# A Mamba-style scan on one Trainium2 core: in the last pair of images VectorE takes five of eight products with C instead of four

## The chip, the cores and the metric

The kernel runs on one core of one Trainium2 chip. The metric is the device time of a run in microseconds; the kernel before has a median of 14022.91 us over three runs (14009.71 to 14023.95). Five engines of the core matter: TensorE (PE in the profile; its weight loads are PEld), VectorE (DVE), ScalarE (ACT), GpSimd (POOL) and SyncE (SP), which here only issues DMAs. Each engine runs its own queue of instructions in a fixed order and waits on semaphores for the others.

## The reference, cut to what matters

Four layers are applied in turn to eight images of 64 channels and 64 x 64 points: a self-attention over points with convolutions, two windowed attention blocks, a decoupled dynamic filter, and a selective scan (SS2D) with a small modulation network behind it. The change lies in the selective scan of the fourth layer. For every image there are K = 4 directions, 128 inner channels, N = 16 states and a sequence of L = 4096 points:

```
def step(h, inp):
    u_t, dt_t, B_t, C_t = inp
    h = h * jnp.exp(dt_t[..., None] * A) + dt_t[..., None] * B_t[:, :, None, :] * u_t[..., None]
    return (h, jnp.einsum('bkcn,bkn->bkc', h, C_t))
```

So each state n has its own recurrence along the points, h = h * exp(dt * A) + (dt * u) * B, and the output is the sum over the states of h * C. B and C depend on the point and the state but not on the channel.

## The kernel before, in words

Channels lie on the 128 partitions. Images are worked in four pairs. The main program (`tile_kernel`, L1838) runs, for each pair, the method `scans` (L1619); between the steps of the scans it takes pieces of other work from a generator: the part behind the scans of the pair before (`back`, L1755) and the layers in front of the scans of the pair to come (`front`). In the last pair there is no pair to come, so only `back` of the third pair is mixed in, and after the last scan its own `back` runs alone.

A pair has two images, four directions and eight chunks of 512 points: 64 units (the list `units`, L1629). A unit has eight steps (`i % 8`), and a step treats two of the 16 states, j = 0 and j = 1. That is 512 steps for a pair and 2048 in all. The scans of the last pair are steps 1536 to 2047; below, unit numbers count from the start of that pair, so that units 0 to 31 are its first image and 32 to 63 its second.

What one step needs, and which engine does it:

- `fetch` (L1677): SP issues a DMA that broadcasts two rows of B, and another for two rows of C, to all partitions, 512 KB each. B is fetched three steps ahead and C two steps ahead. The tiles of B and of C have three buffers each, so a fetch waits until the product that reads the same buffer three steps earlier has ended; SP issues its DMAs strictly in order.
- `products` (L1684), two steps ahead: POOL multiplies both rows of B with dt * u into the tile `vd` (six buffers), one instruction over 128 x 1024 elements (L1687).
- `step` (L1689): for each of the two states ScalarE writes exp(dt * A) into a PSUM bank called `dad` (L1707); VectorE runs the recurrence as one scan instruction over 512 points (L1710), from `dad` and `vd`, into `to`; and ScalarE copies the last point of `to` to `carry` for the next chunk (L1718). `to` is either the SBUF tile `hd` (one buffer for even and one for odd steps) or `dad` itself, in place, so that the state stays in PSUM.
- The product with C, written over `vd`. It has two forms, chosen by `rp` (L1696). Where `rp` is 0 one POOL instruction covers both states (L1721). Elsewhere POOL multiplies the first state, which is in SBUF (L1723), and VectorE the second, which is in PSUM (L1724). In the first three pairs `rp` is set in odd steps; in the last pair (`image >= B - 2`) it is set in every step, so VectorE takes four of every eight products.
- `sums` (L1726): TensorE adds the two products of a step to the output bank `yd` with an identity matrix (L1737); after the eighth step VectorE adds `yd` to the running sum Y (L1746, L1748, L1751).

At the start of each unit `inputs` (L1653) loads the points `xs`, and forms dt and dt * u (`pdd` and `du`; L1662 to L1669) and the rows of B and C (L1671 to L1675), which go to DRAM and come back by `fetch`.

[...]Three are in the pool of the scans under the tag `da` (for `dad`, `pdd` and `pbc`), one is `yd`, three belong to the mixed-in work (tag `f`), and one to its accumulations. `bank` (L1179) hands them out. In the last pair, once the mixed-in work is used up, `turn` is set (L1645) and `bank` alternates between the two pools, so that `dad` rotates through six banks; that is so from unit 32 on.

The order of the instructions on each engine is not written out by hand. A scheduler that orders the whole program when it is built decides it, from priorities and its own estimate of durations; on the chip the order is fixed. So a change of one product can move others.

Of the kernel before, what the change touches and what calls it, by code (L numbers as in the profile page):

```python
# [11 lines left out]
ALU = mybir.AluOpType  # L12
# [3 lines left out]
B, C, HH, WW = 8, 64, 64, 64  # L16
# [9 lines left out]
NTD = L // TD  # L26
# [1121 lines left out]
class _Direct:  # L1148
# [540 lines left out]
    def step(self, i, st):  # L1689

        nc, w, net = self.nc, self.w, self.net
        wk, ps = self.sw, self.ps
        u = self.units[i // 8]
        k, c, at, CC, v = u["k"], u["c"], u["at"], st["C"], st["v"]

        n0, rp = 2 * (i % 8), i % 2 or u["image"] >= B - 2  # L1696
        rev = k >= 2

        def along(t):
            return t[:, ::-1] if rev else t  # L1700

        h = wk.tile([P, 2 - i % 2, TD], F32, name="hd", tag=f"h{i % 2}", bufs=1)
        hs = []
        for j in range(2):
            n = n0 + j
            da = self.bank("dad", (P, TD), "da")
            nc.scalar.activation(da, u["du"][:, 0], AF.Exp, scale=net.As[:, k, n : n + 1])  # L1707
            first = 0.0 if at == 0 else self.carries[:, n : n + 1]
            to = da if rp and j else h[:, j]
            nc.vector.tensor_tensor_scan(along(to), along(da), along(v[:, j]), first, ALU.mult, ALU.add)  # L1710
            hs.append(to)
            if at < NTD - 1 and (rp or j):
                ends = h[:, :, 0] if rev else h[:, :, TD - 1]
                cs = self.carries[:, n0 : n0 + 2]
                if rp:
                    ends = to[:, 0:1] if rev else to[:, TD - 1 : TD]
                    cs = self.carries[:, n : n + 1]
                nc.scalar.activation(cs, ends, AF.Copy)  # L1718

        if rp == 0:  # L1720
            st["w"] = nc.gpsimd.tensor_tensor(v, h, CC, ALU.mult)  # L1721
        else:
            st["w"] = nc.gpsimd.tensor_tensor(v[:, 0], h[:, 0], CC[:, 0], ALU.mult)  # L1723
            nc.vector.tensor_tensor(v[:, 1], hs[1], CC[:, 1], ALU.mult)  # L1724

    def sums(self, i, st, after=None):  # L1726

# [161 lines left out]
```

## Time and profile before

| what | value |
|---|---|
| median of three runs | 14022.91 us |
| the profiled execution's own time | 14012.53 us |
| its span in the profile | 14010.7 us |
| mean granted TensorE clock | 0.862 |
| start of the last pair's first product with B | 11620.8 us |
| start of the next 32 units (second image) | 12710.8 us |
| start of the last product with B | 13745.8 us |

The profile is one execution on the chip. A group of instructions is named by line, engine and operation, then output <- inputs with their sizes, how often it ran, its busy time in us and the mean of one in ns. "<-" behind a group or in a view of waits names what ended the idle time before it. Durations of neighbouring instructions of VectorE and POOL overlap by some tens of nanoseconds, so costs are better read from one start to the next. In a view by stretches of time each row gives the busy time of every engine, the granted clock, the mean busy share of the 16 DMA engines and what they moved.

### The profile page before, as it was taken

What the parts mean: (1) busy time and instruction counts of PE and PEld (TensorE: products, weight loads), DVE (VectorE), ACT (ScalarE), POOL (GpSimd) and SP (SyncE); (2) the same over time, 40 slices, a digit from 0 to 9 for tenths busy, and PEclk for the clock granted to TensorE, in tenths of its full rate; (3) what the DMA queues carried; (4) which work ended last, traced back from release to release, by engine and by line L of the source; (5) the groups of instructions that cost most, each with busy time, mean ns of one, the idle gap of its engine ahead of it and who ended that gap; (6) DMA issues with size and microseconds to landing.
All of it is one profiled execution on the core that took longest, in us unless ns stands there. A gap on an engine that the chain in (4) does not pass through costs nothing. (4 is left out here: it accounts for less than half of the span.)

```text
span 14010.7 us, 141613 instructions
## 1 busy us (share of the span) xinstructions
PE 11364.2 (81%) x46358; PEld 4240.7 (30%) x46358; DVE 8425.0 (60%) x9763; ACT 7041.2 (50%) x15460; POOL 8178.9 (58%) x4111
## 2 busy tenths in 40 slices
PE   9888979978888669988889667997998866666665
PEld 2255222234433222224433222223443222222221
DVE  0222254477766874356675767337666677997875
ACT  5533156556544645555553645555554554454442
POOL 0000046578767765556665685457666688878982
PEclk9966789989889789998899788998888878888887
DMA  0000044456555754445554675335544577878882
GB/s 17 1 1 2 6 163 162 159 185 226 195 181 189 246 195 149 135 154 176 176 177 160 227 248 172 131 132 189 173 163 166 183 253 259 273 250 275 276 273 97
DMA packets 705499, 2379.23 MB, mean 170 GB/s; under 512 B 81060, under 2 KB 81188, under 8 KB 703980
## 3 DMA queue, kind: packets, MB, share of 16 engines
q1 hardware_dynamic: 681024, 2315.57, 48.9%
q10 hardware_dynamic: 23724, 54.50, 1.0%
q8 instruction: 367, 6.01, 0.2%
q14 instruction: 384, 3.15, 0.1%
HBM read 2269.08 MB, written 100.66 MB: 169 GB/s over the span
## 5 line engine op out<-in xcount | busy, mean ns | idle before, releaser
L1687 POOL TENSOR_TENSOR vd<-B,du 128x1024 f32<-128x1024 f32 x2048 | 4841.8, 2369 | 3920.1 <-DMA B<-rows 2103.0
L1737 PE MATMUL yd<-vd,pack 128*128 128x512 f32 x8192 | 4625.9, 695 | 1265.4 <-POOL vd L1721 449.5
L1710 DVE TENSOR_TENSOR_SCAN hd<-dad,carry,vd 128x512 f32<-128x512 f32 x2464 | 3093.2, 1271 | 1146.2 <-ACT dad L1707 669.9
L1707 ACT ACTIVATE dad<-du,As 128x512 f32<-128x512 f32 x4096 | 2718.4, 680 | 1017.3 <-DVE hd L1710 701.9
L1737 PEld LDWEIGHTS yd<-vd,pack 128*128 128x128 f32 x8192 | 1624.1, 215 | 3956.6 <-issue 1863.1
L1721 POOL TENSOR_TENSOR vd<-hd,C 128x1024 f32<-128x1024 f32 x768 | 1811.7, 2359 | 1324.0 <-DVE hd L1710 695.7
L1723 POOL TENSOR_TENSOR vd<-hd,C 128x512 f32<-128x512 f32 x1280 | 1637.0, 1280 | 317.9 <-DVE hd L1710 230.0
L1277 ACT ACTIVATE e<-s 128x512 f32<-128x512 f32 x2048 | 1199.2, 591 | 1030.1 <-PE s L1271 1028.6
L1710 DVE TENSOR_TENSOR_SCAN dad<-dad,carry,vd 128x512 f32<-128x512 f32 x1120 | 1427.6, 1275 | 126.5 <-POOL vd L1687 77.5
L1271 PE MATMUL s<-X 64*128 64x512 f32 x4096 | 1343.5, 647 | 105.5 <-ACT e L1277 105.3
L1263 PE MATMUL po<-e,VT 128*64 128x512 f32 x4096 | 1155.4, 631 | 19.0 <-ACT e L1277 19.0
L1718 ACT ACTIVATE carry<-hd 128x1 f32<-128x1 f32 (+1 forms) x1792 | 357.3, 201 | 1225.9 <-DVE hd L1710 1215.5
L1724 DVE TENSOR_TENSOR vd<-dad,C 128x512 f32<-128x512 f32 x1280 | 860.9, 673 | 72.7 <-ACT carry L1718 62.4
L1425 PEld LDWEIGHTS w_av<-vals,w_e 64*64 64x64 f32 x16384 | 630.9, 163 | 204.5 <-ACT w_e L1415 99.4
L1425 PE MATMUL w_av<-vals,w_e 64*64 64x9 f32 x16384 | 658.6, 218 | 38.2 <-ACT w_e L1415 38.0
L1271 PEld LDWEIGHTS s<-X 64*128 64x128 f32 x4096 | 363.5, 187 | 1052.4 <-issue 823.7
L1710 DVE TENSOR_TENSOR_SCAN hd<-dad,vd 128x512 f32<-128x512 f32 x352 | 420.1, 1211 | 191.7 <-ACT dad L1707 88.3
L1748 DVE TENSOR_TENSOR Y<-Y,yd 128x512 f32<-128x512 f32 x128 | 124.8, 975 | 661.3 <-PE yd L1737 661.1
L1718 ACT ACTIVATE carry<-dad 128x1 f32<-128x1 f32 x1120 | 189.5, 169 | 616.6 <-DVE dad L1710 614.4
L1415 ACT ACTIVATE w_e<-w_e 128x512 f32<-128x512 f32 x512 | 310.8, 627 | 360.7 <-DVE w_e L1410 239.4
L1410 DVE TENSOR_TENSOR w_e<-w_s,bias 128x512 f32<-128x512 f32 x512 | 328.8, 682 | 236.3 <-PE w_s L1398 235.3
L1263 PEld LDWEIGHTS po<-e,VT 128*64 128x64 f32 x4096 | 212.9, 136 | 824.6 <-issue 581.0
(247 smaller groups left out, 11150.5 us busy)
## 6 DMA issues: line engine op xcount, KB each, us to landing
B<-rows SPq DMA_DIRECT2D x2048, 512.0 KB, 5.0
C<-rows SPq DMA_DIRECT2D x2048, 512.0 KB, 4.5
xs<-xt SPq DMA_DIRECT2D x128, 256.0 KB, 2.9
xs<-xc SPq DMA_DIRECT2D x128, 256.0 KB, 3.4
xc<-xcv ACTq DMA_DIRECT2D x64, 256.0 KB, 3.8
zs<-z ACTq DMA_DIRECT2D x64, 256.0 KB, 3.8
xt<-XT ACTq DMA_DIRECT2D x32, 512.0 KB, 7.8
rows<-bc SPq DMA_DIRECT2D x256, 64.0 KB, 2.0
```

The source lines that it names most:

```text
L1263: nc.tensor.matmul(po[half[im]], lhsT=VT[:, t, half[im]], rhs=es[im], start=(t == 0), stop=(t == 31))
L1271: nc.tensor.matmul(ss[im], lhsT=at(half[im], t), rhs=X[half[im], jc * CH : (jc + 1) * CH], start=True, stop=True)
L1277: nc.scalar.activation(e, ss[im], AF.Exp, scale=C**-0.5, accum_out=parts[:, im, t, jc : jc + 1])
L1425: nc.tensor.matmul(self.av[half[im], x % 4 + j, h, :], lhsT=es[h // 4][half[im], j, h % 4, :], rhs=V[half[im], x + j, h, :], start=True, s ...
L1687: self.nc.gpsimd.tensor_tensor(v, st["B"], dx.to_broadcast([P, 2, TD]), ALU.mult)
L1707: nc.scalar.activation(da, u["du"][:, 0], AF.Exp, scale=net.As[:, k, n : n + 1])
L1710: nc.vector.tensor_tensor_scan(along(to), along(da), along(v[:, j]), first, ALU.mult, ALU.add)
L1718: nc.scalar.activation(cs, ends, AF.Copy)
L1721: st["w"] = nc.gpsimd.tensor_tensor(v, h, CC, ALU.mult)
L1723: st["w"] = nc.gpsimd.tensor_tensor(v[:, 0], h[:, 0], CC[:, 0], ALU.mult)
L1724: nc.vector.tensor_tensor(v[:, 1], hs[1], CC[:, 1], ALU.mult)
L1737: m = nc.tensor.matmul(y, lhsT=w["ident"], rhs=st["v"][:, j], start=(n == 0), stop=(n == NST - 1))
```

## The change

The test is no longer a yes or no for the whole step but the number of the step's states that VectorE multiplies, `own`. In the first three pairs it is 0 in even and 1 in odd steps, as `rp` was. In the last pair it is 1 in three of four steps and 2 in every fourth (i % 4 == 3). Where it is 2, both scans write in place into their PSUM banks, both carries are copied from there, and VectorE does both products with C; POOL does none in that step, and the tile `hd` of the step is allocated but not written. So VectorE takes five of every eight products. Everything outside `step` is the same. In the changed program each engine's instructions stand in the same order as before up to the start of the last pair's scans.

```
-        n0, rp = 2 * (i % 8), i % 2 or u["image"] >= B - 2
+        n0 = 2 * (i % 8)
+        own = 1 + (i % 4 == 3) if u["image"] >= B - 2 else i % 2
...
-            to = da if rp and j else h[:, j]
+            to = da if j >= 2 - own else h[:, j]
             nc.vector.tensor_tensor_scan(along(to), along(da), along(v[:, j]), first, ALU.mult, ALU.add)
             hs.append(to)
-            if at < NTD - 1 and (rp or j):
+            if at < NTD - 1 and (own or j):
                 ends = h[:, :, 0] if rev else h[:, :, TD - 1]
                 cs = self.carries[:, n0 : n0 + 2]
-                if rp:
+                if own:
...
-        if rp == 0:
+        if own == 0:
             st["w"] = nc.gpsimd.tensor_tensor(v, h, CC, ALU.mult)
-        else:
-            st["w"] = nc.gpsimd.tensor_tensor(v[:, 0], h[:, 0], CC[:, 0], ALU.mult)
-            nc.vector.tensor_tensor(v[:, 1], hs[1], CC[:, 1], ALU.mult)
+        for j in range(2 if own else 0):
+            engine = nc.vector if j >= 2 - own else nc.gpsimd
+            m = engine.tensor_tensor(v[:, j], hs[j], CC[:, j], ALU.mult)
+            if j == 0:
+                st["w"] = m
```

## The prediction

> **What bounds the kernel now.** I read the page first. The shares of the whole span name TensorE, but the slices show that the last sixth is another regime.
>
> ```profile
> PE 11364.2 (81%) x46358; PEld 4240.7 (30%) x46358; DVE 8425.0 (60%) x9763; ACT 7041.2 (50%) x15460; POOL 8178.9 (58%) x4111
> ...
> POOL 0000046578767765556665685457666688878982
> ```
>
> The eights and nines at the end of POOL's row are the last pair's scans. Its 512 steps begin at 11620.8 and end near 13748: 2127 us, the only part where the two programs' order differs. There I asked for the busy time by stretch, cut where the products with B of step 8u start. Columns: stretch, its length, PE, PEld, DVE, ACT, POOL busy, clock, DMA share, GB/s.
>
> ```profile
> 11620.80:12139.30 518.50, 363.94 (x662) 120.61 (x662) 435.70 (x445) 265.37 (x618) 455.70 (x255) 0.89 0.81 279
> 12139.30:12552.40 413.10, 278.90 (x474) 93.73 (x473) 391.57 (x431) 218.11 (x445) 323.12 (x179) 0.81 0.69 239
> 12552.40:12740.00 187.60, 121.89 (x216) 39.44 (x216) 151.84 (x158) 88.25 (x209) 170.35 (x97) 0.88 0.85 294
> 12740.00:12983.60 243.60, 156.77 (x257) 53.90 (x257) 183.29 (x186) 105.36 (x247) 200.47 (x115) 0.80 0.76 256
> 12983.60:13748.20 764.60, 493.44 (x852) 171.75 (x852) 610.40 (x620) 346.88 (x831) 678.93 (x382) 0.85 0.81 275
> 13296.00:13330.50 34.50, 20.90 (x33) 7.21 (x34) 27.41 (x29) 15.90 (x40) 28.45 (x18) 0.80 0.73 240
> 13330.50:13358.70 28.20, 18.63 (x40) 6.46 (x38) 23.51 (x24) 14.00 (x35) 28.20 (x16) 1.00 0.96 322
> ```
>
> The last two rows are two neighbouring units of eight steps. The second is solid POOL: 28.20 of 28.20. The first does the same work in 34.5 us. The static order explains it: in one unit VectorE takes each step's two scans in turn ("straight"); in the other it runs the second states' scans of steps 2 to 6 ahead of the first states' ("crossed"), so POOL's product with C of step 2 stands waiting. The second image's 24 units from 12983.6 on are 12 of each: 12 x 34.4 + 12 x 28.25 = 752, and 13 us more among the last eight.
>
> The timeline of a straight stretch, POOL and then VectorE (start, duration):
>
> ```profile
> 13344.61 2.36 POOL L1687 TENSOR_TENSOR vd<-B,du 128x1024 f32<-128x1024 f32 x1
> 13346.93 1.27 POOL L1723 TENSOR_TENSOR vd<-hd,C 128x512 f32<-128x512 f32 x1
> 13348.15 2.37 POOL L1687 TENSOR_TENSOR vd<-B,du 128x1024 f32<-128x1024 f32 x1
> ```
>
> ```profile
> 13347.01 1.28 DVE L1710 TENSOR_TENSOR_SCAN hd<-dad,carry,vd 128x512 f32<-128x512 f32 x1 [0.46 <-POOL vd L1687]
> 13348.21 0.67 DVE L1724 TENSOR_TENSOR vd<-dad,C 128x512 f32<-128x512 f32 x1
> 13348.79 1.28 DVE L1710 TENSOR_TENSOR_SCAN dad<-dad,carry,vd 128x512 f32<-128x512 f32 x1
> ```
>
> From start to start a product with B takes 2.31, one with C on POOL 1.22, a scan 1.19, VectorE's product 0.59. A step costs POOL 3.53 and VectorE 2.97; VectorE waits 0.46 for POOL. And in the crossed unit, POOL alone:
>
> ```profile
> 13311.92 2.36 POOL L1687 TENSOR_TENSOR vd<-B,du 128x1024 f32<-128x1024 f32 x1 [0.70 <-DMA B<-rows]
> 13316.90 1.27 POOL L1723 TENSOR_TENSOR vd<-hd,C 128x512 f32<-128x512 f32 x1 [2.62 <-issue]
> ...
> 13327.94 1.27 POOL L1723 TENSOR_TENSOR vd<-hd,C 128x512 f32<-128x512 f32 x1 [1.27 <-DMA C<-rows]
> 13330.48 2.34 POOL L1687 TENSOR_TENSOR vd<-B,du 128x1024 f32<-128x1024 f32 x1 [1.27 <-PE yd L1737]
> ```
>
> With a wait of 0.18 these idle 6.0 us, the 34.5 less 28.45. The last is put down to TensorE, but the fetch of that B was issued at 13324.44, and 6 us is what such a fetch takes here; I read it as the DMA's. That issue stood on SP's queue behind a C fetch that waited for the product of 13322.7 to free its buffer.
>
> **What the Trainium skill says.** "GPSIMD Engine Reference", Elementwise: GpSimd's fp32 tensor_tensor takes 1.96 times VectorE's. The page's rows agree: 1280 ns against 673. "SBUF — State Buffer", SBUF: two separate sides: VectorE with two SBUF inputs and GpSimd exclude each other from a port pair for a whole instruction. The trace agrees: L1830's product of two SBUF tiles took 2.52 us at 12332.97, under a POOL product of 2.35. The moved product reads its state in PSUM, so it should keep 0.67 as L1724 does. "DMA: Bandwidth & Descriptors", Specifications, gives about 358 GB/s of HBM per core; the straight unit runs at 322 with the queues 96% busy, though slices of it reach 424, so measurement puts the ceiling higher. "Perfetto Trace Analysis", Identifying the Most-Contended Engine, calls DMA occupancy misleading; with 158 to 424 GB/s in slices that are all nearly full, it is so here.
>
> **The change, part by part.** (1) In 128 of 512 steps POOL's product goes: 128 x 1.22 = 156 us of POOL, 2.44 per unit. (2) VectorE gets it: 128 x 0.59 = 76 us, 1.18 per unit. Its cover is the 0.46 wait per step; where VectorE has none, all 76 count. (3) The scan of these steps writes PSUM in place: 1281 ns against 1271 on the rows of both forms, 1.3 us in all, nothing. (4) Two PSUM banks are held until the products. The exponential of the next step's second state then follows the first product (0.67 + 0.69) while only one 0.59 product covers it: some 0.25 us per four steps where three banks rotate (the first image, 64 times, 16 us if VectorE bound). In the second image `bank` alternates between two pools, six banks, and it is free. (5) No DMA is added. On SP, C of step 4k+6 waits for VectorE's second product of step 4k+3, and B of step 4k+8 is queued behind.
>
> Straight unit, by hand over four steps: POOL 4 x 2.31 + 3 x 1.22 = 12.9. VectorE 8 x 1.19 + 5 x 0.59 = 12.5, plus half of the unit's two other operations of 0.59 = 13.1. So VectorE becomes the limit by a hair: 26.1 per unit against 28.25. The bytes of a unit, about 8.8 MB, then need 337 GB/s. I take 26.5.
>
> Crossed unit: one product with C is gone before the crossing (1.22). Within it, laid out from the same durations: POOL's first product with C still waits for the fourth B, VectorE does 0.59 more, but the C and B fetches at the end no longer wait for POOL's product of step 3: they go out when VectorE has done it, 19.1 us after the crossing's first B instead of 21.0. The unit's end moves 1.9. Sum 3.1: 34.4 becomes 31.3.
>
> And the scheduler's order changes: in the changed program's last 24 units 8 are crossed and 16 straight; the seven units before stay crossed. The first image has none in either.
>
> Sum. Last 24 units: 8 x 31.3 + 16 x 26.5 + 13 = 687, from 764.6: -77. Of these, four units becoming straight give 25. The seven before: -22. First image: its first 16 units have both engines near (436 and 456); POOL-bound units gain 2, those with the earlier pair's last layer lose 1.2: 0. The 11 units of the second stretch are VectorE bound (392 of 413): +11. The next six: -1.3 each, -8. Total -96. The profiled execution took 14012.53 (span 14010.7), so 13916; it is 10 below the median of the three runs shown. Against that median, 13927; I take **13925**.
>
> **Rivals.** *POOL's full price* (chance 0.13): every straight and first-image unit gains its 2.44: -156, 13867. For: POOL is the only engine solid for 28 us. Against: VectorE's 13.1.
>
> *DMA holds the straight units* (0.15): at 96% share nothing moves faster than 28.2. Then four units turn straight (25) and 15 crossed ones shorten by 3.1 (47): 13951. For: the share. Against: slices of 424 GB/s.
>
> *VectorE was the real limit* (0.07): the first image pays 1.2 us and 0.5 of bank stalls in each of 32 units, 54, and the second gains only that of the four units and half of the shortening: about 14023, no change. For: 95% in one stretch. Against: in the whole pair VectorE is busy 1775 us, and of its idle time 241 us wait for POOL.
>
> *Slower* (0.04): the loop through SP. VectorE's second product of step 4k+3, then two issues (0.35), the landing L, B's product 2.31, scan 1.2, two products 1.26: L + 5.2 per four steps. With L = 5.8, the median in the straight unit, it is 11.0 and hidden. It decides against the change from L = 8.9, where it equals today's 14.1; the longest I saw was 9.3, after a crossing. At 9.9, 1 us is lost in each of the second image's 64 groups: 14087.
>
> That the change does not do what it says can be excluded: POOL's queue has 128 products fewer, VectorE's 128 more.
>
> **How the numbers follow.** My own case has 0.61, with 13885 to 13965: straight units 26.1 to 27.5 (23 us), crossed ones give 1 to 4 (30 us), the first image -15 to +25. The range takes in the full price below and most of the no-change case above: 13862 to 13998. A measurement of this kernel tells about 0.2%, 28 us. Faster: 0.61 + 0.13 + 0.15 = 0.89. Same 0.07, slower 0.04.
>
> **What would show it.** Straight units of 26 to 27 us with VectorE, not POOL, nearly solid; 16 of them among the last 24; crossed ones of 31 to 32; L1687's wait for B's DMA no longer than now; the second stretch (from 12139) a dozen us longer. VectorE's product at 0.67 in both forms: 2 us would mean the port. It is wrong if straight units stay at 28 with DMA above 0.97, or if POOL waits for B in the middle of one.

## The result, and the profile after

The changed kernel takes 13960.18 us (median of 9 runs) against 14019.5 us for the kernel before (9 runs): a ratio of 0.9955, 95% interval 0.9942 to 0.9968, so some 63 us or 0.45% faster. The prediction, 13925 against 14023, was 98 us.

The profiled execution has a span of 13966.9 us, 43.8 less than the one before. From the page after:

```profile
PE 11352.7 (81%) x46358; PEld 4219.7 (30%) x46358; DVE 8487.6 (61%) x9891; ACT 7051.9 (50%) x15460; POOL 8024.8 (57%) x3983
...
POOL 0000045578776765556665685556666677878882
```

POOL has 128 instructions and 154 us less, VectorE 128 more and 63 us more, where parts (1) and (2) of the sum had 156 and 76. Busy time by stretch, cut at the same units as before (stretch, its length, PE, PEld, DVE, ACT, POOL busy, clock, DMA share, GB/s):

```profile
13403.80:13430.20 26.40, 19.05 (x36) 6.48 (x36) 26.09 (x29) 14.84 (x37) 25.90 (x15) 0.94 0.95 326
13430.20:13461.00 30.80, 19.39 (x35) 6.16 (x36) 26.97 (x30) 13.34 (x23) 25.98 (x15) 0.89 0.72 265
11630.20:12163.20 533.00, 381.05 (x669) 121.79 (x668) 456.24 (x480) 270.29 (x620) 420.41 (x225) 0.88 0.80 273
12163.20:12575.70 412.50, 272.10 (x458) 88.45 (x458) 394.09 (x437) 212.80 (x436) 295.73 (x155) 0.82 0.70 238
12575.70:12772.10 196.40, 130.62 (x224) 42.20 (x224) 166.08 (x182) 97.42 (x216) 156.31 (x86) 0.87 0.81 280
12772.10:13003.90 231.80, 150.35 (x252) 50.12 (x253) 188.65 (x199) 104.69 (x245) 182.41 (x99) 0.85 0.79 272
13003.90:13702.00 698.10, 479.87 (x858) 161.11 (x856) 632.76 (x670) 348.82 (x832) 622.24 (x335) 0.89 0.86 302
```

The first two rows are a straight and a crossed unit. The straight one takes 26.4 us instead of 28.2, and VectorE's busy time nearly fills it (26.09), with POOL close behind (25.90). The crossed one takes 30.8 instead of 34.5. The other rows are the five stretches of the pair:

| stretch | before, us | after, us | difference | predicted |
|---|---|---|---|---|
| units 0 to 15 | 518.5 | 533.0 | +14.5 | 0 |
| units 16 to 26 | 413.1 | 412.5 | -0.6 | +11 |
| units 27 to 32 | 187.6 | 196.4 | +8.8 | -8 |
| units 33 to 39 | 243.6 | 231.8 | -11.8 | -22 |
| units 40 to 63 | 764.6 | 698.1 | -66.5 | -77 |
| the five | 2127.4 | 2071.8 | -55.6 | -96 |

The pair begins 9.4 us later than in the execution before, and what follows it takes 2.4 us more; with -55.6 these make the 43.8. The instructions up to the pair stand in the same order in both programs, so the 9.4 is not of the change: it is of the size of the scatter between executions (the 9 runs of before lie between 13987 and 14048). Image by image, the first loses (1090.0 to 1109.4) and the second gains (1037.4 to 962.3).

The waits tell why the two images differ. VectorE's in the first image of the kernel before (who waited for whom; us in all, times, longest):

```profile
DVE du L1668 <- ACT pdd L1667: 49.3, 16, 9.1
...
DVE hd L1710 <- POOL vd L1687: 19.4, 34, 4.0
...
DVE hd L1710 <- POOL vd L1723: 3.2, 4, 1.4
```

and of POOL in the first image of the kernel after:

```profile
POOL vd L1725 <- DVE hd L1711: 195.4, 96, 9.1
POOL vd L1687 <- DMA B<-rows: 73.6, 44, 14.1
```

In the first image only 22.6 us of VectorE's idle time waited for POOL; the other 218 us that I cited for the pair lie in the second (kernel before):

```profile
DVE hd L1710 <- POOL vd L1687: 107.8, 111, 3.5
DVE dad L1710 <- POOL vd L1687: 90.7, 76, 3.0
DVE hd L1710 <- POOL vd L1723: 20.1, 19, 1.2
```

The cover for the first image's 38 us of new products (64 of 0.59) was not there. In the second image it was.

### The profile page after: what moved, and what is told of

Its sections match the earlier page's. It is cut to its first block, busy times and chain, and to the rows that moved or that the text cites. A ratio compares the mean times of both kernels' runs of the same rounds, so it can differ in the third digit from the quotient of the medians.

```text
span 13966.9 us, 141355 instructions
## 1 busy us (share of the span) xinstructions
PE 11352.7 (81%) x46358; PEld 4219.7 (30%) x46358; DVE 8487.6 (61%) x9891; ACT 7051.9 (50%) x15460; POOL 8024.8 (57%) x3983
## 5 line engine op out<-in xcount | busy, mean ns | idle before, releaser
L1711 DVE TENSOR_TENSOR_SCAN hd<-dad,carry,vd 128x512 f32<-128x512 f32 x2352 | 2949.0, 1270 | 1041.4 <-ACT dad L1708 667.6
L1725 POOL TENSOR_TENSOR vd<-hd,C 128x512 f32<-128x512 f32 x1152 | 1476.3, 1282 | 358.7 <-DVE hd L1711 307.5
L1711 DVE TENSOR_TENSOR_SCAN dad<-dad,carry,vd 128x512 f32<-128x512 f32 x1232 | 1560.7, 1273 | 137.3 <-POOL vd L1687 75.5
L1725 DVE TENSOR_TENSOR vd<-dad,C 128x512 f32<-128x512 f32 x1408 | 938.4, 673 | 71.2 <-ACT carry L1719 62.2
L1662 PE MATMUL pdd<-xs,xdt 128*128 128x512 f32 x512 | 329.8, 731 | 190.1 <-DVE hd L1711 78.9
```

Of the source, the lines that this page charges most:

```text
L1662: nc.tensor.matmul(pd, lhsT=net.xdt[:, k, :], rhs=x, start=True, stop=True)
L1725: m = engine.tensor_tensor(v[:, j], hs[j], CC[:, j], ALU.mult)
```

## The experiments

**The change in one image at a time.** In the diffs below the kernel after, or the run named, is the "-" side.

```
-        own = 1 + (i % 4 == 3) if u["image"] >= B - 2 else i % 2
+        own = 1 + (i % 4 == 3 and u["image"] == B - 2) if u["image"] >= B - 2 else i % 2
```

> The change in the last pair's first image alone (units 0 to 31); the second image keeps four of eight products on VectorE, and its order of scans is that of the kernel before (19 crossed units). My prediction's sum has +3 us for this image. Theory now, from the trace after: VectorE has only 23 us of waiting for POOL in this image to hide 38 us of products, so the image is 15 to 20 us longer and the run 10 to 25 us slower than before (ratio 1.0007 to 1.0018). Rival: the 19 us seen in the one trace are chance of that execution, and the ratio is 1.000.

Measured: 14037.1 us, ratio to before 1.0013 (1.0007 to 1.0020), some 18 us slower. In its profile the first image takes 1100.2 us, 10 more than before, and the second 1037.2, as before.

```
+        own = 1 + (i % 4 == 3 and u["image"] == B - 1) if u["image"] >= B - 2 else i % 2
```

> The change in the second image alone (units 32 to 63), whose order of scans is that of the changed kernel (15 crossed units besides the start). Theory: all of the gain is here, 75 us in the traces, and the first image no longer pays, so the run is 70 to 85 us faster than before (ratio 0.9940 to 0.9950), some 15 us faster than the full change. Rival, the first image does not matter: as the full change, 55 to 60 us (ratio 0.9955 to 0.9960).

Measured: 13951.64 us, ratio 0.9952 (0.9939 to 0.9965), 67 us faster. Its second image takes 962.1 us, as in the full change, its first 1092.8. So the whole gain is the second image's, and the first image's loss is real. The traces of the other runs agree: with four of eight the first image takes 1088 to 1096 us in five traces, with five of eight 1100 to 1111 in four, 14 more in the mean. Whether dropping it helps by the 15 us expected isn't separated by these intervals (0.9952 against 0.9955).

**The order alone.** The kernel before, with one edit that changes no operation: in the second image the scan of a step's second state is put behind that of its first in VectorE's queue, so that every unit is straight.

```
-            nc.vector.tensor_tensor_scan(along(to), along(da), along(v[:, j]), first, ALU.mult, ALU.add)
+            s = nc.vector.tensor_tensor_scan(along(to), along(da), along(v[:, j]), first, ALU.mult, ALU.add)
+            if j and u["image"] >= B - 1:
+                net.behind(s, s0)
+            s0 = s
```

> The kernel before with one edit: in the second image the scan of a step's second state is ordered behind that of its first, so no unit is crossed; all products stay where they were. Theory, crossing itself costs the 6 us per unit between 34.4 and 28.25: 19 units give 100 to 120 us (ratio 0.9915 to 0.9930), every unit of the second image takes 28 to 29 us and POOL is solid. Rival: the crossed order only shows a stall that comes anyway from the start of a unit (exponential, logarithm and fetch of the new rows), and the straight order waits in another place: 0 to 30 us.

Measured: 13937.1 us, ratio 0.9947 (0.9934 to 0.9961). Without moving a single product this gains as much as the whole change. The second image takes 957.5 us, 80 less than before. That is less than the 100 to 120 us expected and more than the 30 of the rival: the units are not all of 28 us.

```profile
13252.10:13282.70 30.60, 23.20 (x43) 8.06 (x41) 29.56 (x31) 16.65 (x43) 29.50 (x18) 0.89 0.91 322
13282.70:13311.00 28.30, 18.73 (x36) 6.72 (x36) 25.54 (x27) 14.68 (x37) 28.30 (x18) 0.94 0.93 292
13311.00:13339.80 28.80, 17.59 (x27) 5.81 (x28) 20.93 (x23) 13.19 (x32) 27.00 (x16) 0.77 0.85 281
```

These are three neighbouring units of that run. POOL's 29.50, 28.30 and 27.00 us add up to the work of three units, which the borders, cut at the products with B, share out unevenly; it idles 2.9 us in the three, where a crossed and a straight unit of the kernel before have 6 us between them. Units 33 to 63 average 29.97 us; in the kernel before they average 34.9 crossed (19 of them) and 28.75 straight (12).

The rival holds in part: some of the stall moved to another place. In the second image VectorE's waits for POOL fall from 218.6 to 63.8 us, but it now waits for ScalarE, mostly for dt at the start of a unit; before, such waits came to 0.4 us. Of this run, besides 22.4 us for exponentials:

```profile
DVE du L1668 <- ACT pdd L1667: 56.2, 16, 7.3
```

**Both.** The same edit on the changed kernel.

> The changed kernel with the same edit: no unit of the second image is crossed. Theory: the units that remain crossed (15) fall from 31 to 35 us to 27, so 75 to 95 us more than the change itself: 13865 to 13885, ratio 0.9895 to 0.9910. Against the kernel before with straight units it then wins only the 1.3 us per unit of POOL's relief less what the first image pays: 15 to 35 us. If instead the change's worth is POOL's full price in every unit, the two straight kernels differ by 60 us or more.

Measured: 13934.35 us, ratio 0.9942 (0.9929 to 0.9955). That is some 20 us below the changed kernel, where 75 to 95 were expected. Against the straight kernel before, the two medians differ by 3 us, where 15 to 35 were expected: with the order out of the way the change is worth nothing that these runs can tell. The profiles show two halves that cancel: the second image 935.6 us against 957.5 (22 less; units 33 to 63 average 29.17), the first 1102.1 against 1088.0 (14 more).

**The best of both.** Straight units, and the change in the second image alone.

> Straight units, and the change in the second image alone. Theory: the second image keeps the 935.6 us of the straight changed kernel, the first goes back from 1102 to about 1089: 10 to 15 us faster than with the change in both images, 100 faster than before, ratio 0.9925 to 0.9940. Rival, the two do not add: no faster than the straight kernel before (0.9947).

Measured: 13920.9 us, ratio 0.9933 (0.9919 to 0.9947), with 1095.8 and 929.2 us for the two images. It is the lowest median of the runs that do all of the work, 100 us below before and inside the expected range. It is below the changed kernel too, though the two intervals overlap a little. With the interval of the straight kernel before it overlaps by half, so against that kernel no gain is shown.

**The other half of the change: both states in PSUM.** VectorE takes both products in every fourth step, but the first state stays in the SBUF tile.

```
-            to = da if j >= 2 - own else h[:, j]
+            to = da if j and own else h[:, j]
```

> The change without its second half: in every fourth step VectorE takes both products, but the first state stays in the SBUF tile, so that product reads two SBUF tiles. Theory, [...]from the one product of this kind in the trace before (2.52 us under a POOL product): VectorE and POOL exclude each other, the 128 products take 1 to 2.5 us where POOL is busy instead of 0.67, VectorE loses about 100 us more, and the gain of the change goes: 0 to 60 us slower than the changed kernel. Rival: VectorE starts such a product in POOL's gaps and it stays near 0.7 us; then as the changed kernel within 15 us.

Measured: 14059.28 us, ratio 1.0027 (1.0015 to 1.0039), some 100 us slower than the changed kernel. That is more than I had expected of the run (60), while the loss on VectorE is as expected. Products with C of this run's pair on VectorE, by their inputs (count, busy us, mean ns of one):

```profile
L1725 DVE TENSOR_TENSOR vd<-dad,C 128x512 f32<-128x512 f32 x516 | 344.9, 668 | 0.9 <-ACT carry L1719 0.9
L1725 DVE TENSOR_TENSOR vd<-hd,C 128x512 f32<-128x512 f32 x128 | 188.5, 1473 | 0.0
```

The same product is 0.67 us with its state in PSUM and 1.47 on average with it in SBUF: 128 x 0.80 = 103 us. The Trainium skill, "SBUF — State Buffer", SBUF: two separate sides, says that a VectorE instruction with two SBUF inputs and a GpSimd instruction that reads SBUF exclude each other, each for its whole length. The trace agrees: 100 of the 128 products started under a running POOL instruction and ended some 0.55 us after it; where none was left running (27) they took 0.66 to 0.68. The in-place scan that avoids this costs next to nothing (1277 ns against 1266 in the changed kernel), so the PSUM half is what makes the move worth while. The order in this run is the scheduler's own again, so not all of the 100 us need be the product's.

**Do the DMA engines hold the straight units?** Straight units with the change in both images; in the second image the fetch of C brings one row and both products use it, so the second states' C is left out.

```
+        if s and self.units[i // 8]["image"] == B - 1:
+            row = self.units[i // 8]["rows"][n]
+            self.nc.sync.dma_start(t[:, 0], row.unsqueeze(0).to_broadcast([P, TD]))
+            return
...
-            m = engine.tensor_tensor(v[:, j], hs[j], CC[:, j], ALU.mult)
+            m = engine.tensor_tensor(v[:, j], hs[j], CC[:, j * (u["image"] < B - 1)], ALU.mult)
```

> The changed kernel with straight units, but in the second image the fetch of C brings one row, 256 KB instead of 512, and both products use it (the rows of the second states' C are left out). A quarter of the fetched bytes goes. Its second image stands against 935.6 us of the straight changed kernel. If the DMA engines hold the straight units (my rival in the prediction, and POOL's 66 us of waits for B), the second image falls to 880 to 905 us. If VectorE does, with its own work and its waits for ScalarE, 925 to 940 us.

Measured, in one execution: the second image takes 911.7 us instead of 935.6. Neither theory was right. The last 24 units of the straight changed kernel and of this run:

```profile
12958.20:13649.80 691.60, 476.90 (x863) 157.28 (x861) 635.12 (x676) 348.26 (x834) 622.51 (x337) 0.91 0.87 305
```

```profile
12980.60:13650.70 670.10, 467.07 (x864) 158.30 (x864) 630.62 (x674) 352.45 (x836) 622.48 (x337) 0.92 0.73 239
```

With the DMA share down from 0.87 to 0.73, 21.5 us of 691.6 go. VectorE's busy time then fills 94% instead of 92%. Transfers are a part of what is left over VectorE's own work, somewhat over a third of 56 us; they are not the main thing that holds the units. In the second image VectorE's waits for POOL fall from 19.5 us to 1.2, while those for ScalarE stay, 63.6 and 66.8. The longest item (44.0 in the straight changed kernel):

```profile
DVE du L1668 <- ACT pdd L1667: 44.9, 15, 6.5
```

So with fewer bytes nearly all that is left is VectorE's own work and its waits for ScalarE.

**Further in the same direction.** Straight, the change in the second image alone, and there six of eight on VectorE.

```
+        own = 1 + (i % 2 and u["image"] == B - 1) if u["image"] >= B - 2 else i % 2
```

> Straight units, the change in the second image alone, and there VectorE takes six of eight products (both in every odd step) instead of five. Its second image stands against 929 to 936 us. By hand VectorE then has 27.3 us of work per unit and POOL 23.4. If VectorE limits the second image at five of eight, this costs 0.6 to 1.2 us per unit, so 950 to 975 us, and the run is 20 to 45 us slower than the five of eight. If the fetches of B limit it, POOL's relief changes nothing and the second image stays within 8 us.

Measured: 13932.98 us, ratio 0.9928 (0.9911 to 0.9945); second image 941.6 us. Against the 929 us of the run with five of eight that differs in nothing else it stands between the two expectations; against 936 it is inside the second. As a whole run it can't be told from five of eight. In its last 24 units VectorE is busy 661.07 of 699.10 us (95%), POOL only 565.89: POOL is now far from being the limit, and the time still doesn't fall: 699.1 us against 684.6 to 695.1 in the four traces of straight units with five of eight, 0.2 to 0.6 us more per unit. So between four and six of eight the optimum is flat within what these runs tell.

**The other direction in the first image.** Straight, five of eight in the second image, and three of eight in the first: in every fourth step POOL takes both products in one instruction. The run that it stands beside is the best of both, above.

```
+        own = (1 + (i % 4 == 3) if u["image"] == B - 1 else 1 - (i % 4 == 2)) if u["image"] >= B - 2 else i % 2
```

> As the run beside it, and in the first image VectorE gives a product back: three of eight instead of four (in every fourth step POOL takes both states in one instruction). Theory, VectorE limits the first image: 5 to 15 us faster than the run beside it. Rival, the first image is held by chains through ScalarE and TensorE or by both engines alike: no faster, or up to 20 us slower, as POOL gets 2.3 us per unit more.

Measured: 13998.72 us, ratio 0.9990 (0.9982 to 0.9998); its first image takes 1161.9 us, 66 more than in the run beside it, and the median is 78 us higher. My theory for the first image falls in that form, VectorE doesn't simply limit it; and the loss is far above the 20 us that the rival allowed. POOL's waits there have a new head, at L1725, which in this run is the product of both states (where the profile shows no releaser it says "issue"; us in all, times, longest):

```profile
POOL vd L1725 <- issue: 104.9, 22, 11.4
```

That product can start only when both scans of its step have ended. The edit so changed the shape of the product and the order of the queues along with the share. It tells that this form of three of eight is worse than four, not which of these makes it so bad.

**More banks for the first image.** Straight in both images, and the two pools of PSUM banks shared from the start of the last pair.

```
-                if p == B // 2 - 1 and done >= cost:
+                if p == B // 2 - 1:
```

> The changed kernel, straight in both images, with the two pools of PSUM banks shared from the start of the last pair, so the first image's exponentials rotate through six banks too. It stands against 1102 us for the first image of the straight changed kernel and 1088 of the straight kernel before. If the first image pays for banks held until the products (my estimate was at most 16 us; waits of VectorE's scans for the exponentials grew by only 6), it falls to 1085 to 1095. If it pays for VectorE's products alone, it stays at 1098 to 1106.

Measured: 13984.25 us, ratio 0.9968 (0.9959 to 0.9978); the run is 36 us above the straight changed kernel by the ratios, 50 by the medians. In the profiled execution, the slowest of ten, the first image takes 1153.6 us, longer than either theory said, and POOL waits 125 us for B's fetches there. I read it as the price of the mixed-in work now sharing its banks with the scans; that isn't shown, as the edit holds the order in the first image too. The run doesn't decide whether held banks are a part of the first image's loss; that stays open.

## Why the prediction was right, and where it was off

The direction and the range held; the size was about 1.5 times the measured one. In the traces the pair gained 56 us instead of 96. Of the 40 missing, 20 belong to the first image's three stretches, 10 to the crossed units 33 to 39 and 11 to the last 24. The range was wide, but it did not take in most of the no-change case as its text says: 13998 is below 14023. And the terms of the rival "VectorE was the real limit" add up to 14029 rather than 14023.

*Straight units, 26.5.* In units 40 to 55 the ten straight ones average 26.8 us, from 28.3. The size came out, the reason given for it only in part. That VectorE alone is the limit isn't shown: over the ten units it idles 1.0 us per unit, as POOL does, and nearly all of that behind POOL's products with B. One sign of being wrong that the prediction named did come: within eight of the ten POOL waits for B, between 0.2 and 1.6 us, 7.0 us together. The longest of them:

```profile
13151.15 2.36 POOL L1687 TENSOR_TENSOR vd<-B,du 128x1024 f32<-128x1024 f32 x1 [1.64 <-DMA B<-rows]
```

In the second image SP's waits for VectorE's products went from 270.6 to 391.0 us, the wait that part (5) named; how much of B's lateness comes from it no run shows. The rival "POOL's full price" (28.25 less 2.44, 25.8 per unit) falls; no straight unit here is faster than 26.1. The rival "DMA holds the straight units" falls too: they run below 28.2 with a share of 0.95, and a quarter fewer bytes make the last 24 units of the straight kernel only 3% shorter.

*Crossed units, 31.3.* In units 40 to 55 the six crossed ones average 31.5. The shape of the crossing is as described: the timeline of POOL in such a unit after,

```profile
13445.13 2.35 POOL L1687 TENSOR_TENSOR vd<-B,du 128x1024 f32<-128x1024 f32 x1 [0.88 <-DMA B<-rows]
13450.10 1.27 POOL L1725 TENSOR_TENSOR vd<-hd,C 128x512 f32<-128x512 f32 x1 [2.62 <-issue]
...
13456.90 2.49 POOL L1725 TENSOR_TENSOR vd<-hd,C 128x512 f32<-128x512 f32 x2 [0.92 <-DVE hd L1711]
13459.80 1.27 POOL L1725 TENSOR_TENSOR vd<-hd,C 128x512 f32<-128x512 f32 x1 [0.40 <-DVE hd L1711]
13461.02 2.35 POOL L1687 TENSOR_TENSOR vd<-B,du 128x1024 f32<-128x1024 f32 x1
```

has the same 2.62 us at the first product with C, a wait of 0.92 for VectorE, and none for the fetches at the end, which cost 2 x 1.27 before. Where crossed units follow each other (33 to 39) they came down from 34.8 only to 33.1, not to 31.6: there the term was mis-sized by 10 us. The last eight units of the pair take 241 us (before 264), and the two crossed ones among them take 35.

*The first image, +3.* This step failed. Its terms were -2 for units that POOL bounds and +1.2 for those that VectorE bounds, with a count of each from busy shares; the profile has +23 over its three stretches (the last one reaches one unit into the second image), and the run with the change there alone is 18 us slower (10 to 28). The stretch with the highest share of VectorE, 95%, which I had charged with +11, lost nothing; the stretches where both engines looked equally busy lost 14.5 and 8.8. A busy share over 16 units didn't tell who waits for whom in each. The view of waits of this image alone does: 22.6 us of cover for 38 us of work gives +15. The prediction read that view over the whole pair and quoted 241. Not all of the cover was used: 7.3 us of such waits are left in the kernel after. And the banks held until the products, up to 16 us in part (4) and nothing in the sum, may show too: VectorE's scans wait 26.5 us for exponentials instead of 20.9.

*The order.* The prediction put 25 us of the second image's gain down to four crossed units turning straight. The runs say more than that: with the crossings taken away in both kernels, the change is worth 3 us of the median, within what the runs can tell. Of the 75 us in the second image the moved products are worth 22 where all units are straight (11 to 28 over the four traces with five of eight); the rest is fewer and shorter crossings, and the straight order alone gives 80. The mechanism was in the prediction, but its weight in the verdict was not: I treated shorter crossings as a worth of moving products, and never asked what the crossing itself would be worth.

The "slower" rival, the loop through SP, didn't happen: in the second image POOL's waits for B went from 39.1 to 57.7 us, 19 more where the rival charged 64. By these 19 us the sign "no longer than now" failed.

## What to carry to other kernels

Before moving work from a full engine to another, look whether the full engine is full all the time: here, in the last 24 units, it was solid in half of them and idle for 6 us in each of the others, for an order of instructions that one ordering edge removes, and that edge alone gained as much as the change. Then look where the stall goes: of the 117 us that 19 crossed units cost over straight ones the edge gave 79, since VectorE now waited for ScalarE. Price the cover of moved work in each regime apart, by the waits of that regime: a sum over a stretch that mixes two regimes put the cover where it was not needed. And when an edit makes a scheduler choose another order, run the same edit with the order held, or the gain of the order is booked to the edit.

## What the runs showed of the hardware that I had not expected

A VectorE product of two SBUF tiles beside a busy GpSimd isn't a fixed price: over 128 of them it ran from 0.66 to 2.83 us, mean 1.47, and 100 of them ended 0.55 us after the GpSimd instruction under which they started; the same product with one input in PSUM stayed between 0.65 and 0.71 in all 1280 cases of that run. And a quarter fewer fetched bytes at a DMA share of 0.87 moved the time by only 3%: in that run the share was mostly not a limit.
